# Adding negated row maxima to attention scores by accumulating DMAs, in 8 of 32 units of a cross-attention block

## The chip, the cores and the metric

The kernel runs on one core of a Trainium2 chip. The core has TensorE (PE), VectorE (DVE), ScalarE (ACT), GpSimd (POOL), the sync engine (SP), which here issues every DMA, and 16 DMA engines. The metric is the device time of one execution in microseconds (us), lower is better. All arithmetic is in float32.

## The reference

One transformer block with cross-attention over 8 sequences of 256 tokens, width 512, 16 heads of 32, and a context of 256 tokens for each sequence:

```python
x = layer_norm(hidden_states, ln1_w, ln1_b)
q = (x @ q_w + q_b)                      # split into 16 heads of 32
k = (encoder_hidden_states @ k_w + k_b)
v = (encoder_hidden_states @ v_w + v_b)
scores = einsum('bhqd,bhkd->bhqk', q, k) / sqrt(32)
scores = where(mask, scores, finfo.min)
attn = softmax(scores, axis=-1)
out = einsum('bhqk,bhkd->bhqd', attn, v) @ cproj_w + cproj_b
hidden = out + residual
y = gelu(layer_norm(hidden, ln2_w, ln2_b) @ fc_w + fc_b)
return hidden + (y @ proj_w + proj_b)
```

The part that matters here is the softmax: for each query and head the largest score over the 256 keys is subtracted before the exponential.

## The kernel before

The 8 sequences are worked in two groups (g = 0, 1) of four. Each group goes through the projections of context and tokens, the attention, the output projection, a second layer norm and the two large matrix products of the MLP. The projections and the MLP use recursive 2 x 2 block products with sums of blocks, so DVE and POOL compute many block sums (names such as `c1t`, `x1t`, `ows`, `pw0i`, `y0i`) that feed TensorE.

Attention is cut into 32 units. A unit is named by three digits: group, quarter of the heads (4 heads each), sequence within the group; unit 010 is group 0, head quarter 1, sequence 0. A unit goes through `scores` and `attend`:

- `s` (PE): 8 products give the scores of 4 heads, keys on the 128 partitions in two chunks, 256 queries in the free dimension.
- `ev` (ACT, L619): 8 evictions from PSUM, which also add the mask, into two tiles `pr0` and `pr1` of 128 x 1024 floats, two heads each. One tile of 512 KB is called a half below.
- `mx` (DVE, L1022), `mt` (DVE), `mc` (3 copies on ACT, L1029), `fold` (DVE, L1030): the maxima over the keys, which lie across partitions, end as 32 x 32 numbers (4 heads x 256 queries).
- `md` (SP, L1033): a store of these 4 KB to DRAM.
- `mm` (SP, L1035): a load that repeats the 1024 maxima on all 128 partitions, 128 x 1024 floats, 512 KB.
- `less` (L1038 to L1048): for each half, scores minus maxima in place; on POOL as two instructions of 128 x 512 (L1047), or on DVE as one of 128 x 1024 (L1042).
- `exp` (ACT, L1050): one exponential per half, in place.
- `av` (PE): products of the exponentials with ones (the denominators) and with the values; then DVE normalises.

What is executed in which order is written out by hand. `PROGRAM` is a list of some thousands of words, one for each step, such as `less010_0:G`: the step's name and, after the colon, the engine where there is a choice (V is DVE, A is ACT, G is POOL). The steps are issued in this order, so that on each engine, and on SP's queue, instructions stand in the order of the list and none overtakes another. `PLACES` gives each buffer its slot in SBUF or bank in PSUM. An exponential that waits on ACT therefore holds up every eviction behind it, and a wait on POOL or SP everything behind that. A unit's `av` stands about three units behind its `s` in TensorE's order.

Of the kernel before, what the change touches and what calls it, by code (L numbers as in the profile page):

```python
# [13 lines left out]
ALU = mybir.AluOpType  # L14
PSUM = bass.MemoryType.PSUM

P = 128
# [105 lines left out]

PROGRAM = """
# [42 lines left out]
less010_0:G stats_x1_30 mc012_2 k1_0_P4 k1_0_c12:A mm030 r002 mc012_1 kd0_1_11 mc012_3 ev032_21 mx032_0 ev032_30  # L167
k1_1_P2 ev032_31 less010_1:G ev032_20 k1_0_c21 exp010_0 fold012 k1_1_P3 mx032_1 md012 vd0_1_21 exp010_1 aggr_x1_30
# [8 lines left out]
r030 exp032_1 xb1_21 xb1_20 v1_1_t2:A att030 s003 less012_1:V v1_0_t2:A mm001 av032 xb1_01 mx021_0 ev003_20  # L177
ev003_11 xb1_22 ev003_21 xb1_23 ev003_10 mt021 ev003_00 v1_0_P5 ev003_31 r032 exp012_0 att032 ev003_30 mc021_1
v1_1_P5 mx003_1 mc021_2 ev003_01 less001_0:G mc021_3 exp012_1 fold021 s023 v1_0_c11 md021 v1_1_t3:A mx003_0 xb1_13
av012 xb1_10 ev023_00 less001_1:G ev023_01 mt003 v1_0_t3:V ev023_31 ev023_21 mc003_2 v1_0_P7 mc003_3 r012 ev023_20  # L180
ev023_30 mc003_1 ev023_10 att012 ev023_11 xT1_20 s011 exp001_0 fold003 mx023_0 md003 v1_1_P2 ev011_00 mm021
ev011_31 xb1_12 ev011_11 ev011_20 xb1_11 exp001_1 v1_1_P3 xb1_03 v1_1_c11 ev011_30 mx023_1 ev011_01 ev011_21
v1_0_P3 ev011_10 mt023 xT1_21 x1_20:A mx011_1 mc023_1 x1_21:A less021_1:G s031 mm003 mc023_2 v1_0_c22 mc023_3
v1_0_c12:A xb1_02 mx011_0 av001 xb1_00 ev031_11 ev031_00 less021_0:G mt011 xT1_10 mc011_2 ev031_30 fold023 mc011_3
v1_1_P7 ev031_01 xb1_32 r001 mc011_1 xb1_31 ev031_20 exp021_1 xb1_33 att001 fold011 less003_1:G v1_0_P4 ku033
ev031_31 xT1_11 md023 ev031_21 ev031_10 xb1_30 mx031_1 exp021_0 md011 s013 v1_1_c22 x1_10:A less003_0:G xT1_01
# [17 lines left out]
mx120_1 mm102 s110 o0_0_t1 o0_1_P6 ev110_30 mt120 pw0i1_2:G ev110_31 ev110_11 less100_0:V ev110_20 ev110_21 o0_0_P6  # L204
mc120_2 ev110_10 less100_1:G fold122 ev110_01 mx110_1 mc120_3 mc120_1 ev110_00 s130 o0_1_t2 fold120 pw0i1_4:G
o0_0_P2 ev130_21 o0_0_t2 md120 ev130_10 a0t4:V ev130_20 md122 ev130_11 fl002_0 ev130_01 o0_1_P5 ev130_00 pw0i1_3:V
mm120 exp100_1 mx110_0 ows4:G fl006_2 ev130_30 prd0_1_True o0_0_P5 less102_0:G exp100_0 o0_1_t3 fl001_2 mx130_0
ev130_31 av100 mx130_1 mm122 less102_1:G exp102_0 mt110 mt130 o0_0_t3 mc110_2 s112 mc130_2 r100 mc130_1 mc130_3
mc110_3 o0_1_P3 mc110_1 less120_1:G ev112_11 fold130 ev112_30 o0_0_c11 md130 ev112_31 ev112_21 att100 ev112_20
fold110 o0_0_P3 ev112_01 o0_1_c12 md110 ev112_10 less120_0:G ev112_00 mx112_1 pw0_01_00 exp102_1 o0_1_P7 mm130  # L210
o0_0_c12 exp120_1 mx112_0 less122_0:G mm110 exp120_0 o0_0_P7 o0_1_c22 stats_y0_31 hd3 mt112 s132 mc112_2 o0_0_c22
mc112_1 less122_1:G mc112_3 stats_y0_20 o0_1_P4 ev132_00 aggr_y0_31 fold112 ev132_11 stats_y0_30 ev132_31 md112
# [22 lines left out]
fc016_P2 y0i2_1:G fl002_3 fc012_c11 mm103 fc016_P6 pw0i5_2:G fc016_c11 fl002_1 y0i2_2:G fc002_t1 fc006_P6 pw0i5_4:G  # L235
mx123_0 s111 pw0i3_2:G prd0_5_True mx123_1 pw0i3_3:G fc002_P6 ev111_01 fl006_3 less121_1:G ev111_11 fc006_t2
ev111_10 fc012_P6 mt123 fc016_t2 mc123_3 fc002_P2 ev111_00 fc002_t2 mc123_2 fc006_P5 fl012_3 less121_0:V exp121_1
fc016_P5 mc123_1 fc002_c11 pw0i3_4:G exp121_0 fl006_1 fc002_P5 fold123 y0i6_3:G mx111_0 fc002_P7 md123 less103_0:G
prd0_3_True av121 fc012_t2 fl007_2 fc006_t3 fc016_t3 mm123 y0i2_4:G fc012_P5 fl015_0 fc002_t3 ev111_31 y0i6_4:G
ev111_30 fc002_c22 ev111_21 fc006_P3 less103_1:G ev111_20 exp103_0 mx111_1 fc006_P7 fc002_P4 mt111 fc006_c12  # L240
# [134 lines left out]
mm001=54 av030=2 r030=10 rc030=3 ku021=12 s021_0=1 s021_1=3 s021_2=4 s021_3=0 pr021_0=2 pr021_1=50 mx021=0 mm021=18  # L375
# [136 lines left out]
def tile_xattn_block(  # L512
# [59 lines left out]
    def at(b, i, n=1, w=256):  # L572

        return tile_of(b)[:, i * w : (i + n) * w]
# [42 lines left out]
    def copy(name, dst, src, to, of_, n, bias):  # L617
        T.op(name, [("ACT", 0.356 if n == 256 else 0.57)], [src, (cols, None)], [dst],
             lambda e: nc.scalar.activation(to(), of_(), AF.Identity, bias=bias(), scale=1.0))  # L619
# [389 lines left out]
    def scores(g, hg, b, halves):  # L1009
        u, q, k, v = operands_of(g, hg, b)  # L1010
        sb = [Buf(f"s{u}_{j}", "C", 2) for j in range(4)]
        mm(f"s{u}", 1.076, [(q[0], None), (k[0], None)], [(s, None) for s in sb], [
            (lambda kc=kc, j=j: at(sb[j], kc), lambda kc=kc, j=j: row(k, j)[:, ts(kc, P)], lambda j=j: row(q, j), True)
            for kc in range(2) for j in range(4)], mode="row")
        pr = [Buf(f"pr{u}_{h}", "Q", 4) for h in range(2)]
        for kc in range(2):
            for j in range(4):
                copy(f"ev{u}_{j}{kc}", (pr[j // 2], [2 * (j % 2) + kc]), (sb[j], [kc]), lambda j=j, kc=kc: at(pr[j // 2], 2 * (j % 2) + kc),
                     lambda j=j, kc=kc: at(sb[j], kc), 256, lambda kc=kc: col(2 * (4 * g + b) + kc))
        mx = Buf(f"mx{u}", "mx", 7)  # L1020
# [5 lines left out]
        T.op(f"mt{u}", [("DVE", 0.15)], [(mx, [0, 1])], [(mx, [2])], lambda e: nc.vector.transpose(tile_of(mx)[:, 64:128], tile_of(mx)[:, 0:64]))  # L1026
        for a in range(1, 4):
            T.op(f"mc{u}_{a}", [("ACT", 0.2)], [(mx, [2])], [(mx, [2 + a])],
                 lambda e, a=a: nc.scalar.copy(tile_of(mx)[0:32, 64 + 64 * a : 128 + 64 * a], tile_of(mx)[32 * a : 32 * a + 32, 64:128]))  # L1029
        T.op(f"fold{u}", [("DVE", 0.38)], [(mx, [2, 3, 4, 5])], [(mx, [6])], lambda e: nc.vector.tensor_reduce(  # L1030
            tile_of(mx)[0:32, 320:352], tile_of(mx)[0:32, 64:320].rearrange("p (m c) -> p c m", c=32), axis=mybir.AxisListType.X, op=ALU.max))
        md = dram(f"md{u}", [32, 32])
        store(f"md{u}", md, None, [(mx, [6])], lambda: md.t, lambda: tile_of(mx)[:32, 320:352], 0.01)  # L1033
        M = Buf(f"mm{u}", "Q")
        load(f"mm{u}", M, None, lambda: tile_of(M), lambda: md.t.rearrange("a r -> (a r)").partition_broadcast(P), 0.5, src=[(md, None)])  # L1035
        ss = Buf(f"ss{u}", "Q", 2) if halves else None
        for h in range(2):
            def less(e, h=h):  # L1038
                if e == "DVE":
                    p_ = tile_of(pr[h]).rearrange("p (i k q) -> p i k q", i=2, k=2)  # L1040
                    m_ = tile_of(M)[:, 512 * h : 512 * h + 512].rearrange("p (i q) -> p i q", i=2)
                    nc.vector.tensor_tensor(p_, p_, m_[:, :, None, :].to_broadcast([P, 2, 2, S]), ALU.subtract)  # L1042
                    return
                for i in range(2):
                    j = 2 * h + i
                    p_ = at(pr[h], i, 1, 512).rearrange("p (k q) -> p k q", k=2)
                    E[e].tensor_tensor(p_, p_, at(M, j)[:, None, :].to_broadcast([P, 2, S]), ALU.subtract)  # L1047
            T.op(f"less{u}_{h}", [("POOL", 2.448), ("DVE", 1.16)], [(pr[h], None), (M, None)], [(pr[h], None)], less, lock=True, pieces=2)  # L1048
            T.op(f"exp{u}_{h}", [("ACT", 0.947)], [(pr[h], None)], [(pr[h], None)],
                 lambda e, h=h: nc.scalar.activation(tile_of(pr[h]), tile_of(pr[h]), AF.Exp), table="exp")  # L1050
            if halves:
                two = lambda h=h: tile_of(pr[h]).rearrange("p (i k q) -> p i k q", i=2, k=2)
                plus(f"ss{u}_{h}", (ss, [h]), (pr[h], None), (pr[h], None), lambda h=h: at(ss, h, 1, 512).rearrange("p (i q) -> p i q", i=2),
                     lambda two=two: two()[:, :, 0, :], lambda two=two: two()[:, :, 1, :], 512, pool_too=True)
        return u, v, pr, ss

    def attend(g, hg, b, u, v, pt, ss):
        av = Buf(f"av{u}", "C")
        if ss:
            sums_ = [(lambda j=j: tile_of(av)[j * HD : (j + 1) * HD, 256:512], lambda: ones, lambda j=j: at(ss, j), True) for j in range(4)]  # L1060
        else:
            sums_ = [(lambda j=j: tile_of(av)[j * HD : (j + 1) * HD, 256:512], lambda: ones,
                      lambda j=j, kc=kc: at(pt[j // 2], 2 * (j % 2) + kc), kc == 0) for kc in range(2) for j in range(4)]
        mm(f"av{u}", 1.36 if ss else 1.72, [(v[0], None)] + ([(ss, None)] if ss else []) + [(p_, None) for p_ in pt], [(av, None)], sums_ + [
            (lambda j=j: tile_of(av)[j * HD : (j + 1) * HD, :256], lambda j=j, kc=kc: v[1]()[:, kc, j * HD : (j + 1) * HD],
             lambda j=j, kc=kc: at(pt[j // 2], 2 * (j % 2) + kc), kc == 0)
# [432 lines left out]
```

## Time and profile before

| | |
|---|---|
| runs of the kernel, us | 663.23 and 663.9, median 663.57 |
| span of the profiled execution, first to last instruction, us | 662.0 |
| median of the runs less that span, us | 1.6 |
| TensorE clock granted, share of full speed | 1.00 |
| `md`: issue on SP, median us | 0.32, 32 times |
| `exp`: 64 on ACT, mean us | 1.07 |

The profile shows one execution; its own time is its span and what lies around it, for which the last difference stands. Its page gives busy time by engine, the chain of work that ended last, and groups of instructions by line and engine with the names of the tiles that they write and read (`pr<-pr,mm` writes `pr` and reads `pr` and `mm`). Rows of a timeline read: start, duration, engine, line, operation, tiles, shapes, how many of them were merged, and in brackets the idle time of the engine before them and what ended it. Rows of a table by windows give a stretch, its length, the busy time and number of instructions of the five compute rows (PEld is TensorE's weight load), the clock, the share of the 16 DMA engines, and GB/s. SPq is SP's queue of DMA issues. The idle time of an engine that nothing waits for costs nothing.

### The profile page before, as it was taken

To read this page: it belongs to the slowest core of one execution; us is meant where nothing else is said; L and a number is where in the kernel's file an instruction comes from. 1 tells how busy PE (TensorE), PEld (TensorE's weight loads), DVE (VectorE), ACT (ScalarE), POOL (GpSimd) and SP (SyncE) were. 2 spreads that over 40 slices of the span, in tenths; PEclk is the share of its full clock that TensorE was granted. 3 is DMA by queue.
4 is the path that set the end of the run, shared out by engine and by line. 5 is a ranking of instruction groups with operands and counts; after the bars stand their busy time and mean duration, and the time that the engine had idled before them with its cause. 6 is when DMAs were issued, how large, how long until landed. Compare 5 with 4: busy or idle time off the path is not lost.

```text
span 662.0 us, 11469 instructions
## 1 busy us (share of the span) xinstructions
PE 654.6 (99%) x3925; PEld 490.0 (74%) x3925; DVE 585.7 (88%) x980; ACT 342.4 (52%) x702; POOL 374.8 (57%) x340
## 2 busy tenths in 40 slices
PE   8999999999999999999999999999999999999997
PEld 7746554477544776777688888888888888888887
DVE  2998799999999999999999998997789787998775
ACT  2046479799999899866995572030020013930000
POOL 1262773646888997699958774423535217720260
PEclk9999999999999999999999999999999999999999
DMA  8999888786574467886878698889978779359366
GB/s 250 311 356 307 211 197 291 267 255 125 144 241 161 144 202 234 263 268 197 266 249 273 198 235 225 289 269 230 195 193 241 190 201 242 93 142 240 106 141 111
DMA packets 206586, 144.84 MB, mean 219 GB/s; under 512 B 117008, under 2 KB 166976, under 8 KB 206528
## 3 DMA queue, kind: packets, MB, share of 16 engines
q1 hardware_dynamic: 206528, 144.11, 76.8%
q8 instruction: 31, 0.51, 0.3%
q14 instruction: 27, 0.22, 0.1%
HBM read 104.10 MB, written 39.98 MB: 218 GB/s over the span
## 4 chain that ended last, share of the span: by engine, by line
PE 92%; DVE 5%; ACT 1%; DMA 1%; issue 0%; SPq 0%; POOL 0%; DVEq 0%; ACTq 0%
PE pd_X L639 15%; PE fc_X L639 14%; PE fc_W L639 8%; PE av L639 7%; PE pd_W L639 7%; PE s L639 4%; PE o_X L639 4%; PE q_X L639 4%; PE k_X L639 4%; PE v_X L639 4%; PE pd_Y L639 4%; PE fc_Y L639 4%; PE q_W L639 2%; PE k_W L639 2%; PE v_W L639 2%; PE o_W L639 2%
## 5 line engine op out<-in xcount | busy, mean ns | idle before, releaser
L1047 POOL TENSOR_TENSOR pr<-pr,mm 128x512 f32<-128x512 f32 x84 | 110.4, 1346 | 22.8 <-DMA mm<-md 9.2
L619 ACT ACTIVATE pr<-s,cols 128x256 f32<-128x256 f32 x256 | 104.5, 482 | 21.8 <-PE s L639 15.8
L1022 DVE TRANSPOSE_TENSOR_REDUCE mx<-pr 128x32 f32<-128x1024 f32 x64 | 77.6, 1223 | 3.3 <-ACT pr L619 3.3
L1227 ACT ACTIVATE h<-h,cols 128x256 f32<-128x256 f32 x128 | 54.1, 498 | 36.7 <-DVE h L630 36.6
L1050 ACT ACTIVATE pr<-pr 128x1024 f32<-128x1024 f32 x64 | 66.9, 1069 | 3.4 <-POOL pr L1047 2.8
L630 DVE TENSOR_TENSOR h<-fc_X,h 128x512 f32<-128x512 f32 x80 | 52.8, 679 | 6.2 <-PE fc_X L639 5.5
L630 DVE TENSOR_TENSOR h<-fc_W,h 128x512 f32<-128x512 f32 x48 | 32.0, 679 | 5.8 <-PE fc_W L639 5.3
L639 PE MATMUL av<-pr,ones 128*32 128x256 f32 x512 | 34.2, 384 | 0.7 <-ACT pr L1050 0.6
L1029 ACT COPY mx<-mx 32x64 f32<-32x64 f32 x96 | 23.1, 243 | 19.8 <-DVE mx L1026 15.8
L1042 DVE TENSOR_TENSOR pr<-pr,mm 128x1024 f32<-128x1024 f32 x22 | 30.8, 1407 | 0.0
L628 POOL TENSOR_TENSOR z1i<-h,z1i 128x512 f32<-128x512 f32 x4 | 5.7, 1440 | 40.4 <-PE pd_X L639 40.4
L639 PEld LDWEIGHTS av<-pr,ones 128*32 128x32 f32 x512 | 14.1, 109 | 18.5 <-issue 6.7
L630 POOL TENSOR_TENSOR h<-h,fl 128x512 f32<-128x512 f32 x9 | 11.5, 1295 | 24.6 <-DVE fl L630 15.0
L639 PE MATMUL fc_W<-y1i,fl 128*128 128x256 f32 x100 | 24.6, 380 | 0.0
L639 PE MATMUL fc_X<-y1i,fl 128*128 128x256 f32 x88 | 21.6, 381 | 0.0
L639 PEld LDWEIGHTS fc_W<-y1i,fl 128*128 128x128 f32 x100 | 18.9, 190 | 2.9 <-DVE h L630 0.3
L639 PE MATMUL pd_W<-z0i,pl 128*128 128x256 f32 x88 | 20.6, 379 | 0.0
L1030 DVE TENSOR_REDUCE mx<-mx 32x32 f32<-32x256 f32 x32 | 18.4, 574 | 1.4 <-ACT mx L1029 1.3
L639 PE MATMUL pd_X<-z0i,pl 128*128 128x256 f32 x80 | 18.9, 379 | 0.0
L606 ACT COPY fl<-fc_X 128x512 f32<-128x512 f32 x6 | 3.5, 580 | 29.5 <-PE fc_X L639 29.2
L639 PEld LDWEIGHTS fc_X<-y1i,fl 128*128 128x128 f32 x88 | 16.6, 190 | 2.6 <-ACT h L606 0.2
L639 PEld LDWEIGHTS pd_W<-z0i,pl 128*128 128x128 f32 x88 | 16.7, 190 | 2.3
(595 smaller groups left out, 1815.6 us busy)
## 6 DMA issues: line engine op xcount, KB each, us to landing
mm<-md SPq DMA_DIRECT2D x32, 512.0 KB, 5.1
pl<-prd SPq DMA_DIRECT2D x47, 256.0 KB, 4.2
fl<-fcd SPq DMA_DIRECT2D x41, 256.0 KB, 4.0
fl<-prd SPq DMA_DIRECT2D x24, 256.0 KB, 3.8
fw<-in_L_xattn_fc_w_dram SPq DMA_DIRECT2D x16, 256.0 KB, 4.9
pw<-in_L_xattn_proj_w_dram SPq DMA_DIRECT2D x32, 128.0 KB, 3.6
hid<-in_x_dram SPq DMA_DIRECT2D x8, 512.0 KB, 4.8
hd<-hid SPq DMA_DIRECT2D x8, 512.0 KB, 3.4
```

What stands on the lines that cost most here:

```text
L606: (nc.scalar.copy if e == "ACT" else nc.vector.tensor_copy)(to(), of_())
L619: lambda e: nc.scalar.activation(to(), of_(), AF.Identity, bias=bias(), scale=1.0))
L628: nc.gpsimd.tensor_tensor(to()[:, ts(k, 512)], in0()[:, ts(k, 512)], in1()[:, ts(k, 512)], op)
L630: E[e].tensor_tensor(to(), in0(), in1(), op)
L639: nc.tensor.matmul(o(), l(), r(), start=first, stop=True, skip_group_check=True)
L1022: T.op(f"mx{u}_{h}", [("DVE", 1.126)], [(pr[h], None)], [(mx, [h])], lambda e, h=h: nc.vector.tensor_reduce(tile_of(mx)[:, 0:64].rearrange ...
L1029: lambda e, a=a: nc.scalar.copy(tile_of(mx)[0:32, 64 + 64 * a : 128 + 64 * a], tile_of(mx)[32 * a : 32 * a + 32, 64:128]))
L1030: T.op(f"fold{u}", [("DVE", 0.38)], [(mx, [2, 3, 4, 5])], [(mx, [6])], lambda e: nc.vector.tensor_reduce(tile_of(mx)[0:32, 320:352], tile_ ...
L1042: nc.vector.tensor_tensor(p_, p_, m_[:, :, None, :].to_broadcast([P, 2, 2, S]), ALU.subtract)
L1047: E[e].tensor_tensor(p_, p_, at(M, j)[:, None, :].to_broadcast([P, 2, S]), ALU.subtract)
L1050: lambda e, h=h: nc.scalar.activation(tile_of(pr[h]), tile_of(pr[h]), AF.Exp), table="exp")
L1227: lambda e, f=f, b=b, c=c: nc.scalar.activation(at(h[f][b], c), at(h[f][b], c), AF.Gelu_apprx_tanh, bias=col(c_fcb + f * 4 + c), scale=1.0 ...
```

## The change

In eight units, named in `ADDING`, the load `mm` is gone and so are the subtractions. In their place POOL issues for each half a DMA that reads 16 of the 32 rows of maxima from DRAM (512 numbers, for two heads), repeated on 128 partitions and for the two key chunks, and adds them to the half in SBUF (`accum_op=ALU.add`). So that adding is right, `fold` now writes negated maxima, and the other 24 units add instead of subtracting. So that 512 numbers in a row fit, a half is ordered by key chunk first and head second (it was head first), in the evictions, the maxima, the exponentials' users and the `less` of all units. All 16 changed `less` steps were on POOL before, and each keeps its place in the list; the eight `mm` words are taken out. Nothing else in `PROGRAM` moves, and `PLACES` stays.

```diff
+ADDING = "010 001 021 003 102 120 122 103".split()
...
-less002_1:V kd0_1_21 mm010 exp002_0 k1_1_P5 mx012_1 kd0_1_22 ev012_11 ku001 exp002_1 att020 av022 mt030 xt1_1
+less002_1:V kd0_1_21  exp002_0 k1_1_P5 mx012_1 kd0_1_22 ev012_11 ku001 exp002_1 att020 av022 mt030 xt1_1
...
-                copy(f"ev{u}_{j}{kc}", (pr[j // 2], [2 * (j % 2) + kc]), (sb[j], [kc]), lambda j=j, kc=kc: at(pr[j // 2], 2 * (j % 2) + kc),
+                copy(f"ev{u}_{j}{kc}", (pr[j // 2], [2 * kc + j % 2]), (sb[j], [kc]), lambda j=j, kc=kc: at(pr[j // 2], 2 * kc + j % 2),
...
-                tile_of(mx)[:, 0:64].rearrange("p (k j q) -> p j k q", k=2, j=4)[:, 2 * h : 2 * h + 2],
+                tile_of(mx)[:, 0:64].rearrange("p (k j q) -> p k j q", k=2, j=4)[:, :, 2 * h : 2 * h + 2],
...
-            tile_of(mx)[0:32, 320:352], tile_of(mx)[0:32, 64:320].rearrange("p (m c) -> p c m", c=32), axis=mybir.AxisListType.X, op=ALU.max))
+            tile_of(mx)[0:32, 320:352], tile_of(mx)[0:32, 64:320].rearrange("p (m c) -> p c m", c=32), axis=mybir.AxisListType.X, op=ALU.max, negate=True))
...
+        adding = u in ADDING
         M = Buf(f"mm{u}", "Q")
-        load(f"mm{u}", M, None, lambda: tile_of(M), lambda: md.t.rearrange("a r -> (a r)").partition_broadcast(P), 0.5, src=[(md, None)])
+        if not adding:
+            load(f"mm{u}", M, None, lambda: tile_of(M), lambda: md.t.rearrange("a r -> (a r)").partition_broadcast(P), 0.5, src=[(md, None)])
...
             def less(e, h=h):
+                m_ = at(M, 2 * h, 2)
                 if e == "DVE":
-                    p_ = tile_of(pr[h]).rearrange("p (i k q) -> p i k q", i=2, k=2)
-                    m_ = tile_of(M)[:, 512 * h : 512 * h + 512].rearrange("p (i q) -> p i q", i=2)
-                    nc.vector.tensor_tensor(p_, p_, m_[:, :, None, :].to_broadcast([P, 2, 2, S]), ALU.subtract)
+                    p_ = tile_of(pr[h]).rearrange("p (k n) -> p k n", k=2)
+                    nc.vector.tensor_tensor(p_, p_, m_[:, None, :].to_broadcast([P, 2, 512]), ALU.add)
                     return
-                for i in range(2):
-                    j = 2 * h + i
-                    p_ = at(pr[h], i, 1, 512).rearrange("p (k q) -> p k q", k=2)
-                    E[e].tensor_tensor(p_, p_, at(M, j)[:, None, :].to_broadcast([P, 2, S]), ALU.subtract)
-            T.op(f"less{u}_{h}", [("POOL", 2.448), ("DVE", 1.16)], [(pr[h], None), (M, None)], [(pr[h], None)], less, lock=True, pieces=2)
+                for k in range(2):
+                    p_ = at(pr[h], k, 1, 512)
+                    E[e].tensor_tensor(p_, p_, m_, ALU.add)
+            def added(e, h=h):
+                m_ = md.t[16 * h : 16 * h + 16].rearrange("a r -> (a r)").partition_broadcast(P)
+                nc.gpsimd.dma_start(tile_of(pr[h]).rearrange("p (k n) -> p k n", k=2), m_[:, None, :].to_broadcast([P, 2, 512]), accum_op=ALU.add)
+            if adding:
+                T.op(f"less{u}_{h}", [("POOL", 1.0)], [(pr[h], None), (md, None)], [(pr[h], None)], added)
+            else:
+                T.op(f"less{u}_{h}", [("POOL", 2.448), ("DVE", 1.16)], [(pr[h], None), (M, None)], [(pr[h], None)], less, lock=True, pieces=2)
```

Two places show what this does to POOL's queue. The numbers behind a tile's name are those of its buffer; `x2` is two instructions. The first place is unit 010 (`pr_0_972`, `pr_1_959`) in group 0: before,

```order
L628 TENSOR_TENSOR c1t_1223<-c_10_966,c1t_1027 128x512 x2
L1047 TENSOR_TENSOR pr_0_972<-pr_0_972,mm_1142 128x512 x2
L1047 TENSOR_TENSOR pr_1_959<-pr_1_959,mm_1142 128x512 x2
L807 TENSOR_TENSOR rs_x_3_1294<-rs_x_3_1294,neg_half 128x2
L1047 TENSOR_TENSOR pr_1_1079<-pr_1_1079,mm_1250 128x512 x2
```

and now:

```order
L628 TENSOR_TENSOR c1t_1221<-c_10_966,c1t_1027 128x512 x2
L1051 DMA pr_0_972<-md_150 128x2x512
L1051 DMA pr_1_959<-md_150 128x2x512
L807 TENSOR_TENSOR rs_x_3_1289<-rs_x_3_1289,neg_half 128x2
L1048 TENSOR_TENSOR pr_1_1079<-pr_1_1079,mm_1247 128x512 x2
```

Four subtractions became two issues at the same place; they still stand behind the sums `c1t`, and wait for `md` instead of `mm`. The second place is POOL at units 102 (`mm_2327`), 120 (`mm_2410`) and 122 (`mm_2449`) in group 1, with units 130 and 110 behind them: before,

```order
L630 TENSOR_TENSOR ows_2414<-v_1_11_299,ows_2202 128x512
L1047 TENSOR_TENSOR pr_0_2216<-pr_0_2216,mm_2327 128x512 x2
L1047 TENSOR_TENSOR pr_1_2170<-pr_1_2170,mm_2327 128x512 x2
L1047 TENSOR_TENSOR pr_1_2299<-pr_1_2299,mm_2410 128x512 x2
L1047 TENSOR_TENSOR pr_0_2286<-pr_0_2286,mm_2410 128x512 x2
L1047 TENSOR_TENSOR pr_0_2111<-pr_0_2111,mm_2449 128x512 x2
L1047 TENSOR_TENSOR pr_1_2115<-pr_1_2115,mm_2449 128x512 x2
L1047 TENSOR_TENSOR pr_0_2395<-pr_0_2395,mm_2519 128x512 x2
L1047 TENSOR_TENSOR pr_1_2391<-pr_1_2391,mm_2519 128x512 x2
```

and now:

```order
L1051 DMA pr_0_2199<-md_189 128x2x512
L1051 DMA pr_1_2153<-md_189 128x2x512
L1051 DMA pr_1_2282<-md_188 128x2x512
L1051 DMA pr_0_2269<-md_188 128x2x512
L1051 DMA pr_0_2094<-md_190 128x2x512
L1051 DMA pr_1_2098<-md_190 128x2x512
L1048 TENSOR_TENSOR pr_0_2376<-pr_0_2376,mm_2492 128x512 x2
L1048 TENSOR_TENSOR pr_1_2372<-pr_1_2372,mm_2492 128x512 x2
```

Six halves are now issued one right behind the other, with no other work of POOL between them.

More of the change, by code (lines that the diff above doesn't have):

```diff
@@ L1051, in scores @@
             if halves:
[L1052 removed]
+                two = lambda h=h: tile_of(pr[h]).rearrange("p (k i q) -> p k i q", i=2, k=2)
                 plus(f"ss{u}_{h}", (ss, [h]), (pr[h], None), (pr[h], None), lambda h=h: at(ss, h, 1, 512).rearrange("p (i q) -> p i q", i=2),
[L1054 removed]
+                     lambda two=two: two()[:, 0], lambda two=two: two()[:, 1], 512, pool_too=True)
         return u, v, pr, ss
@@ L1062, in attend @@
             sums_ = [(lambda j=j: tile_of(av)[j * HD : (j + 1) * HD, 256:512], lambda: ones,
-                      lambda j=j, kc=kc: at(pt[j // 2], 2 * (j % 2) + kc), kc == 0) for kc in range(2) for j in range(4)]
+                      lambda j=j, kc=kc: at(pt[j // 2], 2 * kc + j % 2), kc == 0) for kc in range(2) for j in range(4)]
         mm(f"av{u}", 1.36 if ss else 1.72, [(v[0], None)] + ([(ss, None)] if ss else []) + [(p_, None) for p_ in pt], [(av, None)], sums_ + [
             (lambda j=j: tile_of(av)[j * HD : (j + 1) * HD, :256], lambda j=j, kc=kc: v[1]()[:, kc, j * HD : (j + 1) * HD],
-             lambda j=j, kc=kc: at(pt[j // 2], 2 * (j % 2) + kc), kc == 0)
+             lambda j=j, kc=kc: at(pt[j // 2], 2 * kc + j % 2), kc == 0)
             for kc in range(2) for j in range(4)], mode="col")
```

41 lines of the change are left out of this document (20 added, 21 removed).

## The prediction

> **What bounds the kernel now.** I read the page first: busy times, then the chain that ended last.
>
> ```profile
> span 662.0 us, 11469 instructions
> ...
> PE 654.6 (99%) x3925; PEld 490.0 (74%) x3925; DVE 585.7 (88%) x980; ACT 342.4 (52%) x702; POOL 374.8 (57%) x340
> ...
> PE 92%; DVE 5%; ACT 1%; DMA 1%; issue 0%; SPq 0%; POOL 0%; DVEq 0%; ACTq 0%
> ```
>
> TensorE works 654.6 of 662.0 us and makes 92% of the chain; POOL, from which the change takes work, makes 0%. All that any relief can bring is TensorE's idle time, 662.0 - 654.6 = 7.4 us. So the question is whether something that TensorE waits for comes later. For that I read the stretches in which the eight units run: first all attention from 99 to 265 us, then the four places where the changed units stand, and one stretch with a single load of maxima in it.
>
> ```profile
> core 0: us, PE busy (x) PEld busy (x) DVE busy (x) ACT busy (x) POOL busy (x), PEclk, DMA share, GB/s
> 99.00:265.00 166.00, 164.83 (x1383) 100.50 (x1382) 159.21 (x278) 153.89 (x319) 121.44 (x93) 1.00 0.69 207
> ...
> 218.00:222.00 4.00, 4.00 (x30) 3.04 (x29) 4.00 (x6) 2.70 (x9) 4.00 (x4) 1.00 0.42 131
> 119.00:129.00 10.00, 10.00 (x59) 4.63 (x61) 9.93 (x23) 7.43 (x17) 8.45 (x8) 1.00 0.87 288
> 143.00:170.00 27.00, 26.94 (x259) 18.89 (x261) 24.91 (x43) 26.43 (x59) 14.02 (x12) 1.00 0.72 139
> 228.00:245.00 17.00, 17.00 (x132) 13.06 (x135) 16.81 (x30) 14.47 (x33) 17.00 (x14) 1.00 0.75 233
> 299.00:312.00 13.00, 13.00 (x95) 9.66 (x97) 12.76 (x23) 8.96 (x14) 12.76 (x14) 1.00 0.69 197
> ```
>
> TensorE is idle for 1.2 us of these 166. ACT is busy for 153.9 of them (93%), so ACT cannot make good several us in which it stands at a wait. The second number from the end is the share of the DMA engines: they are no empty road, 0.69 to 0.87 at the four places.
>
> **The change part by part.** The rows of the work that goes, and of the queue that issues it:
>
> ```profile
> L1047 POOL TENSOR_TENSOR pr<-pr,mm x84: 1258/1278/2767, 85.1 to 318.2; 128x512 f32<-128x512 f32 x84
> L593 SPq DMA_DIRECT2D mm<-md x32: 319/344/889, 79.2 to 367.8; - x32
> ...
> DMA to landing us min/median/max: 3.4/5.1/7.2
> ...
> DMA to landing us min/median/max: 3.7/3.7/3.7
> ...
> SPq L593 <- DMA md<-mx: 8.3, 9, 1.9
> ```
>
> *Removed on POOL:* 8 units x 4 subtractions x 1.28 = 41 us. No piece of it is on the chain, and TensorE has no gap behind it: worth 0. *Removed on SP:* 8 issues of 0.34 us and at most the 8.3 us that SP spent at its nine waits for maxima; what was queued behind starts earlier, but TensorE has no gap that it ended: 0. *Changed in the other 24 units:* the order of a score tile, the sign, an add for a subtraction, on the same shapes, one POOL call per key chunk in place of one per head. If each of the 52 POOL calls left took the 0.02 us between minimum and median more or less, that is 1 us on POOL, beside TensorE's work: 0.
>
> *Added:* 16 DMAs, two per unit, each writing half a unit's scores, 128 x 1024 numbers or 512 KB. No row shows an accumulating DMA or one that POOL issues. The nearest is the load it replaces: also 512 KB, from the same small tensor. The one at 218.0 us has the engines almost to itself: it lands after 3.7 us, and 4 us x 0.42 = 1.68 us of that is time of all engines; the other 2.0 are fixed. Bounds for the data time of one adding half: 1.68 us if the add is free, 5.0 us if read, read and write each cost a plain copy. I take 3.36, twice the load, since it must read two sources, maxima and scores, where the load read one. For POOL's issue the ends are SP's 0.34 us and the 2.55 us of the two calls it replaces; I take 1.0, nearer to SP's row, since it is an issue. While other packets are there, an adding packet twice as long that alternates with a plain one takes 1.5 times as long; with a share b of other traffic I multiply by 1 + b/2.
>
> [...] No row of the trace shows an add.
>
> *Unit 010.* POOL comes to it at 119.46, behind sums that waited for ACT; below it ACT's two exponentials, three copies of maxima behind them, and TensorE's use (start, duration, engine, line):
>
> ```profile
> 119.46 4.97 POOL L1047 TENSOR_TENSOR pr<-pr,mm 128x512 f32<-128x512 f32 x4
> ...
> 122.77 1.07 ACT L1050 ACTIVATE pr<-pr 128x1024 f32<-128x1024 f32 x1
> 124.46 1.06 ACT L1050 ACTIVATE pr<-pr 128x1024 f32<-128x1024 f32 x1 [0.62 <-POOL pr L1047]
> 126.08 0.75 ACT L1029 COPY mx<-mx 32x64 f32<-32x64 f32 x3 [0.56 <-DVE mx L1026]
> ...
> 127.87 1.07 PE L639 MATMUL av<-pr,ones 128*32 128x256 f32 x16
> ```
>
> With b = 0.87 a half takes 3.36 x 1.43 = 4.8 us. The first lands at 119.5 + 1.0 + 2.0 + 4.8 = 127.3, the second at 132.1; its exponential ends at 133.2, and TensorE starts 5.3 us late. ACT stands at the first exponential from 122.8 on, and behind it wait the copies for unit 032 and the evictions of the next scores, so later units move with it, not further. Ends: 0 (data as in the load, issue as on SP: ready at 127.7) and 12 (5.0 us of data, 2.55 of issue: 139.5).
>
> *Units 001, 021, 003.* Here POOL waited for the load itself:
>
> ```profile
> 149.31 4.99 POOL L1047 TENSOR_TENSOR pr<-pr,mm 128x512 f32<-128x512 f32 x4 [7.01 <-ACT pr L619]
> 160.52 4.99 POOL L1047 TENSOR_TENSOR pr<-pr,mm 128x512 f32<-128x512 f32 x4 [6.22 <-DMA mm<-md]
> ...
> 143.37 0.49 SPq L593 DMA_DIRECT2D mm<-md  x1
> ...
> 155.18 1.05 ACT L1050 ACTIVATE pr<-pr 128x1024 f32<-128x1024 f32 x1
> ...
> DMA to landing us min/median/max: 2.9/4.5/5.6
> ...
> 172.81 3.66 PE L639 MATMUL q_X<-x,qw 128*128 128x512 f32 x8
> ```
>
> Unit 001's maxima were in DRAM by 143.4, when SP issued the load; POOL was idle and now issues then. The first half lands at 143.4 + 3.0 + 3.36 x 1.27 = 150.7, before its exponential at 155.18; the later two gain their load in the same way: 0. But six halves are 20.2 us of the engines for three loads' 5.0, 15 more in a stretch of 27 that had 7.6 free. With them compete the loads of the normalised tokens (the last landing row, median 4.5 us), whose product starts at 172.81 with nothing idle before it. Between 0 and another 4.5 us I take 2, nearer to 0, since the adds here have room and can be the ones that wait.
>
> *Units 102, 120, 122.* POOL's 18 calls in one row are these units and 130 and 110 behind them:
>
> ```profile
> 227.82 22.28 POOL L1047 TENSOR_TENSOR pr<-pr,mm 128x512 f32<-128x512 f32 x18
> ...
> 230.36 1.06 ACT L1050 ACTIVATE pr<-pr 128x1024 f32<-128x1024 f32 x1 [1.07 <-POOL pr L1047]
> ...
> 235.62 3.22 ACT L1050 ACTIVATE pr<-pr 128x1024 f32<-128x1024 f32 x3
> ...
> 243.71 2.05 ACT L1050 ACTIVATE pr<-pr 128x1024 f32<-128x1024 f32 x2
> ...
> 247.40 1.07 PE L639 MATMUL av<-pr,ones 128*32 128x256 f32 x16
> ```
>
> POOL issues six halves from 227.8 on, faster than they move. They need 20.2 us; the other traffic is 0.75 x 17 less two loads of 1.68, or 0.55. The sixth lands at 227.8 + 3.0 + 20.2 x 1.28 = 256.6, its exponential ends at 257.7, and the product of unit 122, at 247.40 until now, is 10.3 us late. POOL is free 9 us earlier for unit 130, but its exponentials stand behind these on ACT. Ends: 0 and 24, by the same two prices.
>
> *Unit 103.*
>
> ```profile
> 299.34 2.52 POOL L1047 TENSOR_TENSOR pr<-pr,mm 128x512 f32<-128x512 f32 x2
> ...
> 303.20 2.50 POOL L1047 TENSOR_TENSOR pr<-pr,mm 128x512 f32<-128x512 f32 x2
> ...
> 306.47 1.06 ACT L1050 ACTIVATE pr<-pr 128x1024 f32<-128x1024 f32 x1
> ...
> 311.20 1.07 PE L639 MATMUL av<-pr,ones 128*32 128x256 f32 x16
> ```
>
> The halves land at 299.3 + 3.0 + 4.3 = 306.6 and, behind it on the engines, 310.9; the exponential ends at 312.0, 0.8 us late.
>
> Sum: 5.3 + 2 + 10.3 + 0.8 = 18.4, about 19 with the small waits between. The profiled execution spans 662.0; the two runs shown have a median of 663.57, 1.6 more, which I add: 662 + 19 + 1.6 = 682.6, rounded to 682.
>
> **Rivals.** *The transfer is hidden (not slower).* If the add is free, a half is 1.68 us of data. Unit 010 then lands at 124.9 and 127.3, 0.5 late; the six halves are there by 243.7, in time; with ACT standing 2.6 us at 230.4 the sum is about 2: 665.6. It decides at the six halves: they are in time as long as 227.8 + 3.0 + 6 x d x 1.28 stays under 247.4 - 1.1, that is up to d = 2.0 us. For it: the load lands in 5.1 us at the median with other traffic. Against it: scores are read as well. [...]
>
> *Dearer.* Three copies' time (5.0 us) and 2.55 us of POOL per issue: unit 010 ends at 139.5 (12 late), the six halves at 271.9 (24 late), unit 103 at 317.8 (7 late), the token loads 4.5: +47, about 711. For it: no row bounds how fast POOL describes such a transfer. [...]
>
> *A gain.* Freed POOL and SP fill TensorE's gaps: at most the 1.2 us of this stretch if no add comes late: 662.4. Units 001 to 003 are so placed, 010 and 122 are not.
>
> **How the numbers follow.** A measurement of this kernel tells 2% from no change, 650.3 to 676.8. Twice the load (682, its own range 672 to 692): 0.42; hidden: 0.30; dearer: 0.22, spread from 692 to 730; a gain: 0.06. Slower takes the dearer case and four fifths of the likeliest: 0.56. Faster would need more than TensorE's idle time: 0.01. Same: 0.43. The range runs from 662, which leaves out most of the gain (0.05), to 706, which leaves out somewhat over half of the dearer case (0.12).
>
> **What would show it.** In the profile after: a second DMA queue with 16 issues by POOL of about 1 us; their landing, 6 to 8 us for a first half and 4 to 5 more for each one behind it; ACT waiting for DMA before exponentials near 123 and 230; TensorE gaps before the products of units 010 and 122, of some 5 and 10 us; no gap for 001. If those gaps are missing, the data time was under 2.0 us and the kernel stays near 665; if POOL's issue takes over 2 us or a half over 5, it goes to 700 and over.

## The result and the profile after

The kernel after takes 694.7 us (median of two runs, 694.88 and 694.53). Against the kernel before its ratio is 1.047, 95% interval 1.044 to 1.050: slower, by 31 us, where 682 was predicted with a range of 662 to 706. The profiled execution took 694.88 us and spans 693.1, which is 31.1 more than the 662.0 before.

The page of the kernel after: span, busy times, the two DMA queues, and the chain of work that ended last.

```profile
span 693.1 us, 11467 instructions
...
PE 664.2 (96%) x3925; PEld 494.5 (71%) x3925; DVE 590.8 (85%) x980; ACT 343.1 (49%) x702; POOL 355.1 (51%) x324
...
q1 hardware_dynamic: 205376, 139.92, 71.5%
q0 software_dynamic: 4352, 8.39, 7.1%
...
PE 52%; DMA 3%; DVE 2%; POOL 1%; issue 1%; ACT 1%; SPq 0%; POOLq 0%; DVEq 0%; ACTq 0%
```

The chain is no measure of the loss here: it could be followed back only to 280.7 us, so its shares add up to 60% and can't be set against the 92% before. TensorE's busy time rises by 9.6 us, though the trace has the same 3925 of its matmul instructions, and its idle time from 7.4 to 28.9. So about 21.5 of the 31.1 us are idleness, and the rest is slower work. Queue q0 is new: the 16 DMAs of POOL. The next view is TensorE's waits, the longest first (engine, tile and line, what was waited for, total us, times, longest).

```profile
PE av L639 <- ACT pr L1057: 7.3, 4, 3.1
PE q_X L639 <- ACT x L762: 4.6, 1, 4.6
PE o_W L639 <- DVE hid L630: 4.0, 1, 4.0
PE av L639 <- ACT pr L619: 3.3, 2, 2.1
```

The first row is waits of a product `av` for an exponential (L1057 is now the exponential's line). Two of its four, 3.1 and 2.5 us, are the forecast gap of unit 010, and one of 1.2 us is unit 103's; the gap forecast before unit 122's product is not among them. The longest single waits are elsewhere: before the first product of the queries, and before a product `o_W` of the output projection, which reads no scores at all. In the last row 2.1 us are unit 130's. The slower work shows in a table by windows, whose third number from the end is the granted clock.

```profile
130.54:137.37 6.83, 3.81 (x30) 1.55 (x32) 1.72 (x2) 4.29 (x9) 0.00 (x0) 0.50 0.51 160
185.15:191.98 6.83, 5.83 (x7) 2.53 (x8) 6.55 (x11) 6.76 (x15) 5.36 (x4) 0.50 0.59 156
256.83:263.66 6.83, 5.23 (x12) 4.21 (x13) 6.52 (x10) 6.46 (x14) 0.00 (x0) 0.50 1.14 206
```

In three gaps the clock falls to half for 6.83 us; in the kernel before it was 1.00 from 6 us to 661 us. TensorE worked 14.9 us at half clock, so an estimate of the loss is 7.4 of the 9.6 us. Last, the DMAs themselves (issue durations on POOL, who waited, issue to landing) and, in a second view, the loads of the normalised tokens, which took 2.9/4.5/5.6 us to land before.

```profile
L1051 POOL DMA_DIRECT2D pr<-md x16: 1201/1688/3720, 119.5 to 328.1; - x16
...
  ACT pr L1057: 25.0, 7
...
DMA to landing us min/median/max: 6.9/11.3/20.0
```

```profile
L593 SPq DMA_DIRECT2D xb<-xd x16: 331/684/6382, 150.4 to 184.0; - x16
...
DMA to landing us min/median/max: 4.0/8.2/12.6
```

ACT stood 25.0 us at seven exponentials, each time for one of these DMAs. How late TensorE is along the program, by the start of the same product in both timelines:

| product of unit | before | after | later by | added since the row above |
|---|---|---|---|---|
| 030, behind 010 | 136.17 | 144.25 | 8.1 | 8.1 |
| 003 | 176.40 | 192.66 | 16.3 | 8.2 |
| 100 | 229.63 | 247.77 | 18.1 | 1.9 |
| 110, behind 102, 120, 122 | 254.56 | 281.62 | 27.1 | 8.9 |
| 121, ahead of 103 | 300.51 | 327.13 | 26.6 | -0.4 |
| 123, behind 103 | 317.12 | 346.84 | 29.7 | 3.1 |
| end of the span | 662.0 | 693.1 | 31.1 | 1.4 |

Units 010 (first row) and 001, 021 and 003 (second row) were to cost 5.3 and 2, units 102, 120 and 122 10.3, unit 103 0.8.

### The profile page after: what moved, and what is told of

Read it like the earlier page. It is cut to its first block, busy times and chain, and to the rows that moved or that the text cites. A ratio compares the mean times of both kernels' runs of the same rounds, so it can differ in the third digit from the quotient of the medians.

```text
span 693.1 us, 11467 instructions
## 1 busy us (share of the span) xinstructions
PE 664.2 (96%) x3925; PEld 494.5 (71%) x3925; DVE 590.8 (85%) x980; ACT 343.1 (49%) x702; POOL 355.1 (51%) x324
## 3 DMA queue, kind: packets, MB, share of 16 engines
q0 software_dynamic: 4352, 8.39, 7.1%
## 4 chain that ended last, share of the span: by engine, by line
PE 52%; DMA 3%; DVE 2%; POOL 1%; issue 1%; ACT 1%; SPq 0%; POOLq 0%; DVEq 0%; ACTq 0%
PE pd_X L639 14%; PE fc_X L639 11%; PE pd_W L639 7%; PE fc_W L639 6%; PE pd_Y L639 3%; PE fc_Y L639 3%; PE o_X L639 2%; PE av L639 2%; DMA pr<-md 2%; PE o_W L639 1%; PE s L639 1%; DMA mm<-md 1%; PE o_Y L639 1%; ACT pr L1057 0%; POOL y0i L630 0%
## 5 line engine op out<-in xcount | busy, mean ns | idle before, releaser
L1048 POOL TENSOR_TENSOR pr<-pr,mm 128x512 f32<-128x512 f32 x52 | 71.4, 1400 | 33.3 <-DMA mm<-md 28.5
L1057 ACT ACTIVATE pr<-pr 128x1024 f32<-128x1024 f32 x64 | 66.9, 1064 | 26.5 <-DMA pr<-md 25.0
L639 PE MATMUL av<-pr,ones 128*32 128x256 f32 x512 | 36.8, 392 | 10.7 <-ACT pr L1057 7.3
L639 PEld LDWEIGHTS av<-pr,ones 128*32 128x32 f32 x512 | 14.6, 110 | 30.2 <-ACT pr L1057 10.3
L1051 POOL DMA_DIRECT2D pr<-md x16 | 20.2, 1861 | 12.3 <-PE s L639 10.9
```

The source lines that it names most:

```text
L639: nc.tensor.matmul(o(), l(), r(), start=first, stop=True, skip_group_check=True)
L1048: E[e].tensor_tensor(p_, p_, m_, ALU.add)
L1051: nc.gpsimd.dma_start(tile_of(pr[h]).rearrange("p (k n) -> p k n", k=2), m_[:, None, :].to_broadcast([P, 2, 512]), accum_op=ALU.add)
```

## The experiments

The theory is that all of the loss comes from halves that land late, place by place, because a transfer by POOL starts late, halves follow one another in series, other loads wait behind them, and what waits in order on ACT and DVE carries the delay to TensorE, whose clock then falls. Rivals: the new order and sign cost something everywhere; the places make one another worse; the add itself is the whole price. The kernel before, measured beside the experiments, had medians of 664.8 to 666.3 us, with single runs from 662.7 to 673.9, so results are given as ratios to it, and in us as ratio times 663.6.

### The layout alone, and one place at a time

Each of these five kernels differs from the kernel after in which units add by DMA; the others have their load `mm` and their `less` on POOL back, at the places of the kernel before.

```diff
-ADDING = "010 001 021 003 102 120 122 103".split()
+ADDING = "".split()                 # 1: layout and sign alone
+ADDING = "010".split()              # 2
+ADDING = "001 021 003".split()      # 3
+ADDING = "102 120 122".split()      # 4
+ADDING = "103".split()              # 5
```

> No unit adds by DMA: all 32 units load their maxima and add them with POOL or DVE, in the new order of a half and with the new sign. Theory (all of the 31 us comes from the halves that land late): the kernel stands at the time before, 663.6, between 662 and 666, TensorE's clock is 1.00 throughout. Rival (the new order or the sign costs time in the units that don't change, for instance a slower add on POOL, 1.40 us in the kernel after against 1.28 before): at least 668.

> Only unit 010 adds by DMA. Theory (each place pays for its own late landing, read from the kernel after): TensorE is 8 us late behind the product of unit 010, of which 3.2 are a clock of 0.5 for 6.8 us: 671.7, between 670 and 674. Rival (the places make each other worse, a single one is taken up by slack): under 668. By the prediction's term alone: 669.

> Only units 001, 021 and 003 add by DMA. Theory (the token loads share the DMA engines with four adding halves and land 4 us and more later, TensorE waits for them before the product of the queries, and its clock then falls): 672, between 669 and 675, one gap of 3 to 5 us before the first query product. Rival (the waits there come from ACT, already late from unit 010): under 667 without that gap. By the prediction's term alone: 665.6.

> Only units 102, 120 and 122 add by DMA. Theory (ACT stands some 8 us at the first exponential of unit 102, the copies of maxima behind it and DVE's queue stand too, TensorE waits for DVE, then for unit 122): 674, between 671 and 676, with one stretch of clock 0.5. Rival (the delay there is inherited from the two places before it): under 668. By the prediction's term alone: 673.9.

> Only unit 103 adds by DMA. Theory (each place pays for its own late landing; in the kernel after, its second half landed 11.7 us after its issue and TensorE was 3.7 us late from there on): span 666, between 664.5 and 667, ratio 1.005. Rival (what was seen there is inherited from the places ahead): span under 664. By the prediction's term alone: 663.1.

| units that add | ratio, interval | us more than before | TensorE later at the place, by the timelines |
|---|---|---|---|
| none | 1.001 (0.998 to 1.004) | 0.5 | 0 |
| 010 | 1.013 (1.009 to 1.018) | 8.9 | 8.6 |
| 001, 021, 003 | 1.014 (1.009 to 1.018) | 9.0 | 6.1 |
| 102, 120, 122 | 1.013 (1.007 to 1.019) | 8.7 | 8.3 |
| 103 | 1.006 (1.002 to 1.009) | 3.7 | 5.0 |

The last column is by how much TensorE's lateness grows between two products, one ahead of the place and one behind it: 002 and 030, 012 and 003, 100 and 101, and, for unit 103, 121 and the end.

The layout and the sign cost nothing that can be measured. The four places add up to 30.3 us, with intervals of 2 to 4 us each, and the kernel after loses 31.1. So each place pays for itself, and nothing shows that the places make one another worse; a few us of that would not stand out. In the third kernel the time was as expected, but the gap, 2.9 us long, was not before the queries' product but before a `scores` product; that one waited for DVE, and DVE stood 7.4 us at the transposition of the token loads. The token loads landed after 3.2/7.0/15.0 us. (Its two columns differ because the profiled execution, 670.9 us, was the shortest of four, 670.9 to 675.4.) In the fourth the time was as expected too, but behind DVE's 3.3 us TensorE waited 2.6 us before unit 130's product, not for unit 122. The profiled execution of the kernel with 103 alone spans 672.3 us, by a stall at 216 us far ahead of unit 103 (last section); its 5.0 us are counted from behind that stall.

### Two halves fewer beside the token loads

```diff
-ADDING = "001 021 003".split()
+ADDING = "001 021".split()
```

> Only units 001 and 021 add by DMA: the two halves of unit 003 are taken out of the kernel that adds in 001, 021 and 003 (ratio 1.014, span 668.7). Theory (the loads of the normalised tokens wait behind adding halves; with two halves fewer, 5 to 6 us of the engines' time come free before 172): the token loads issued near 160 land within 9 us where two of them took 15 and 11.5, TensorE's gap before the scores at 169.7 is under 1 us, clock 1.00, span 663 to 665. Rival (unit 001 or 021 alone holds ACT or DVE up): 667 or more.

Measured: 1.008 (1.005 to 1.011), 5.2 us; token loads 3.3/7.2/11.2 us; clock 1.00; one gap of 1.2 us before the queries' product, and TensorE 2.9 us later at the place where three units made 6.1. With two halves fewer the delay is smaller, as the theory has it, and the gap before the scores is under 1 us (0.4), but the delay does not go away. The span, 667.3, missed the expected 663 to 665 and lies in the rival's range; 1.5 and 1.0 us of it were lost near 210, where nothing adds.

### A copy in place of the add

```diff
-nc.gpsimd.dma_start(tile_of(pr[h])..., m_..., accum_op=ALU.add)
+nc.gpsimd.dma_start(tile_of(pr[h])..., m_...)
...
-lambda e, h=h: nc.scalar.activation(tile_of(pr[h]), tile_of(pr[h]), AF.Exp), table="exp")
+lambda e, h=h: nc.scalar.activation(tile_of(pr[h]), tile_of(pr[h]), AF.Exp, scale=0.001 if adding else 1.0), table="exp")
```

> The kernel after, all eight units, with the 16 DMAs of POOL copying the maxima over the scores where they added them (the sum of scores and maxima is left out in these units, and their exponentials take a thousandth of the value so that they stay finite; shapes, queues, waits and order are the same). Theory (a half's 2.8 us of data is the add: packets of 2 KB that take 176 ns against 84 for a plain one): packets fall to about 85 ns, halves follow each other by 1.4 us, the last of the six lands some 10 us earlier, and the time falls from 694.7 to about 680, between 674 and 686; what is left of the 31 us is the fixed part of a transfer issued by POOL and the order on ACT. Rival 1 (the software queue sets the pace, the add is free): packets or their spacing stay, 692 to 697. Rival 2 (the fixed part counts for nothing): under 670.

Measured: 1.030 (1.024 to 1.037), or 683.5 us, as expected. The page's row of the software queue and the rows of its issues:

```profile
q0 software_dynamic: 2304, 8.39, 5.0%
...
L1051 POOL DMA_DIRECT2D pr<-md x16: 722/722/867, 120.9 to 321.3; - x16
...
  ACT pr L1057: 20.1, 5
...
DMA to landing us min/median/max: 5.8/10.1/13.3
```

The copy moves a half in 128 packets of 4 KB, the add in 256 of 2 KB. In the packet records a copying packet takes 159 ns undisturbed (169 at the median) and an adding one 176, so by an estimate a half alone is 1.3 us of all 16 engines against 2.8. The six halves of 102, 120 and 122 end 1.3 us apart at the close (landings 256.4, 257.7, 259.0, 260.5) where adding halves ended 2.6 apart, and the last lands 13.3 us after its issue in place of 20.0, or 16.9 us after the first issue in place of 23.6: 6.7 us sooner, not 10. So the add costs an estimated 1.5 us a half, 24 us of the engines in all (by the two pages' shares of the queue, 7.1% of 693.1 us and 5.0% of 685.9, its packets took 49 and 34 us of them, 15 apart), and of the 31 us lost it accounts for 11, or 7 to 15 by the copy's interval. The other 20 stay when the add is gone. Three things are in them that no run separates: the fixed part of the transfer, the waits in order, and the bytes, since two halves of 512 KB are moved for each unit where the load `mm` moved 512 KB once (8.39 MB on the new queue, 4.19 fewer on the old one). Even beside copies the token loads land after 3.1/9.3/11.0 us. By the timelines the places cost 7.8, 4.0, 4.8 and 2.2 us with copies, against 8.1, 8.2, 8.9 and 3.1 with adds. At unit 010 the copy saves next to nothing: its first half still lands 9.6 us after its issue.

### ACT's order at units 102, 120 and 122

The timeline of the kernel after at unit 102's first exponential, ACT first, then DVE and TensorE:

```profile
246.92 0.51 ACT L619 ACTIVATE pr<-s,cols 128x256 f32<-128x256 f32 x1
255.11 1.06 ACT L1057 ACTIVATE pr<-pr 128x1024 f32<-128x1024 f32 x1 [7.68 <-DMA pr<-md]
256.18 1.29 ACT L1029 COPY mx<-mx 32x64 f32<-32x64 f32 x6
...
257.11 0.57 DVE L1030 TENSOR_REDUCE mx<-mx 32x32 f32<-32x256 f32 x1 [5.94 <-ACT mx L1029]
257.61 0.67 DVE L630 TENSOR_TENSOR hid<-o_Y,hid 128x512 f32<-128x512 f32 x1
...
258.43 1.19 PE L639 MATMUL o_W<-qw,a0t 128*128 128x256 f32 x2 [3.99 <-DVE hid L630]
```

ACT waits 7.7 us for the first half of unit 102. Behind it stand six copies of maxima of units 110 and 130, for them DVE's `fold`, behind that a sum that empties a PSUM bank, and for the bank TensorE. Unit 102's own product starts 18 us after its last exponential: nobody was in a hurry for it. Three kernels with 102, 120 and 122 alone change orders. The first moves one exponential:

```diff
-exp102_0 mt110 mt130 ... mc110_1 ... pw0_01_00 exp102_1 ...
+mt110 mt130 ... mc110_1 ... pw0_01_00 exp102_0 exp102_1 ...
```

> Only units 102, 120 and 122 add by DMA, as in the third single-place kernel (672.5, ratio 1.013), and one word is moved: the first exponential of unit 102 goes on ACT behind the copies of maxima of units 110 and 130 and the evictions of unit 112, to the place just before the second one. No DMA is moved. Theory (ACT's order carries the first half's lateness to work that has nothing to do with it): the gap before the product o_W and the low clock there are gone, the maxima of 130 and 110 are loaded 5 us earlier; what stays is unit 122, whose second half lands at 251 for a product due at 247.4: 668, between 666 and 670. Rival (the adds hold up the transfers beside them, not ACT's order): 671 to 674.

Measured: 1.014 (1.010 to 1.018), 672.9 us: no better, and in the rival's range. The gap before `o_W` is gone, and a gap of 6.1 us stands before the scores of unit 101, whose banks wait for evictions behind the exponentials: ACT now waits 0.7, 1.7, 1.6, 2.6 and 2.7 us at five halves. Moved back by itself, the first exponential only shifts ACT's waits to the halves that come 2.6 us apart. The second kernel reorders the issues too:

```diff
-less102_0 less102_1 less120_1 less120_0 less122_0 less122_1
+less122_0 less122_1 less120_1 less120_0 less102_0 less102_1
-exp102_0 (ahead of the copies) exp102_1 exp120_1 exp120_0 exp122_0 exp122_1
+exp122_0 exp122_1 exp120_1 exp120_0 ... exp130_1 exp130_0 exp102_0 exp110_1 exp102_1 exp110_0
```

> Only units 102, 120 and 122 add by DMA, with the six issues on POOL in the order in which TensorE needs the units (122, 120, 102 in place of 102, 120, 122), and the six exponentials in the same order on ACT, none ahead of the copies of maxima of 110 and 130; unit 102's two go behind those of unit 130. Same transfers, same queue. Theory (six halves of 2.6 us in series can be hidden, since unit 102 is needed 16 us after its exponentials): within 2 us of the time before, 664 to 667, no gap above 2 us and no low clock. Rival (the transfers' own length decides, six halves do not fit): 670 or more.

Measured: 1.007 (1.004 to 1.010), 668.4 us. In the profiled execution the clock is 1.00 throughout, and TensorE is 4.7 us later at the place in place of 8.3. So some 3.6 us, nearly half of the place's loss, go by order alone, less than expected. The times agree with that, but their intervals (1.004 to 1.010 and 1.007 to 1.019) overlap, so it rests on the two timelines. The third spreads the exponentials:

```diff
-exp122_0 exp122_1 exp120_1 ... mc112_3 ... exp120_0 ... exp130_1
+exp122_0 ... mc112_3 exp122_1 ... exp120_1 ... exp120_0 exp130_1
```

> Only units 102, 120 and 122 add by DMA, issued in the order of need as in the kernel before of that name (ratio 1.007, span 667.3, ACT idle 3.9 us at exponentials in three waits, then TensorE 2.3 us before the scores of unit 101, whose banks wait for evictions behind these). Now the exponentials stand further apart on ACT: 122's second behind the copies of maxima of 112, 120's first where 122's first stood before, 120's second just ahead of unit 130's. Theory (what remained was ACT standing at halves that follow each other every 2.6 us): ACT's waits for the added halves under 1.5 us, span 664 to 666, left over is unit 102's second half, which lands at 254.5 for a product due at 252.8. Rival (the transfers beside the adds, for units 130 and 110, are what is late): 667 or more.

Measured: 1.007 (1.004 to 1.011), 668.5 us. The waits of that stretch:

```profile
POOL pr L1048 <- DMA mm<-md: 14.1, 2, 11.8
...
PE av L639 <- ACT pr L1057: 3.7, 1, 3.7
ACT pr L619 <- POOL pr L1048: 3.4, 1, 3.4
```

ACT no longer waits for an adding half. Now POOL waits 11.8 us for the maxima of unit 130, ACT for POOL, and TensorE for an exponential that I had put behind that. The load for unit 110 landed 8.8 us after its issue (5.4 in the kernel before). Behind TensorE's gap of 3.7 us the clock was at half for 6.8 us. So the rival's range came true: the loads beside the adds are late too, though part of this wait is the new order's own.

### The clock

> The kernel after, with products that nobody reads put into three of TensorE's idle times: 10 before and 8 in the middle of unit 010's product, 14 before the first product of the queries, some 0.23 us each, with constants as operands. The halves still land when they did. Theory (the clock of 0.5 for 6.8 us behind a gap costs TensorE some 3.2 us each time): the low stretches at 130.5 and 185.2 are gone, the one at 257 stays, and the time falls by about 6 us to 688, between 686 and 691. Rival (the lost clock lies beside other waits, and the added products are more work): 694 to 699.

```diff
+if u == "010":
+    idle = (lambda: tile_of(av)[:, :256], lambda: ident.t, lambda: cb.t[:, :256], True)
+    sums_ = [idle] * 10 + sums_[:2] + [idle] * 8 + sums_[2:]
...
+if name == "q1_0" and p == 1:
+    items = [(lambda: tile_of(bank)[:, :256], lambda: ident.t, lambda: cb.t[:, :256], True)] * 14 + items
```

Measured: 1.052 (1.046 to 1.057). This is the rival's range, but the run tells little: each added product took 0.46 us, twice what I had reckoned, so they outlasted the gaps, and the later gaps moved; the eight in the middle also change unit 010's sums. The low clock at 130 was gone, others came at 180, 242 and 269. So it was tried again on the kernel with unit 010 alone:

```diff
+if u == "010":
+    sums_ = [(lambda: tile_of(av)[:, :256], lambda: ident.t, lambda: cb.t[:, :256], True)] * 12 + sums_
```

> Only unit 010 adds by DMA, as in the first single-place kernel (ratio 1.013, span 670.1, clock 0.5 from 130.4 to 137.2). Added are 12 products of constants that nobody reads, 0.46 us each, ahead of unit 010's product: TensorE starts them where it fell idle (126.8) and is done at about 132.4, still before the second half's exponential (133.6), so nothing real is held up. Theory (the clock that falls behind a gap costs TensorE about 3.3 us): the clock stays 1.00 and the span falls to about 667, between 666 and 668, ratio 1.008. Rival (the low clock costs nothing, since TensorE would wait anyway): span 670 or more.

TensorE behind the second half's exponential, first without the added products, then with them:

```profile
133.65 1.50 PE L639 MATMUL av<-pr,ones 128*32 128x256 f32 x10 [2.74 <-ACT pr L1057]
...
137.21 1.12 PE L639 MATMUL k_W<-c1t,vw 128*128 128x512 f32 x2
```

```profile
127.85 5.45 PE L639 MATMUL av<-cb,ident 128*128 128x256 f32 x24
...
134.42 0.84 PE L639 MATMUL av<-pr,ones 128*32 128x256 f32 x10 [0.56 <-ACT pr L1057]
...
136.27 1.13 PE L639 MATMUL k_W<-c1t,vw 128*128 128x512 f32 x2
```

The rest of unit 010's product takes 1.85 us at full clock against 3.56, so the clock cost 1.7 us here, about half of the 3.8 us that TensorE works in such a stretch, not the 3.3 expected. The clock stays at 1.00, and by the timelines TensorE is 6.6 us late behind the place, where it was 8.6 without them. The time, 1.011 (1.005 to 1.016), does not tell it from the 1.013 without, and the span, 671.0, lies in the rival's range, as the profiled execution lost another 2.5 us near 210. The loss at the other two places, 2.9 and 2.6 us by the same halving, is an estimate that no run tried.

## Why the prediction came out as it did

Right: slower, in the range, by late halves at the places named; removals on POOL and SP worth nothing; layout and sign worth nothing (1.001). A POOL issue of 1.0 us was near: 1.2 to 1.3 for the first of a row, and 0.7 to 0.9 from the start of one to the next (the longer durations in the view overlap). The data of a half, twice a plain copy, holds: 2.8 us where 3.36 was taken, and 2.2 times the copy by the same queue.

Alone the four places cost 8.9, 9.0, 8.7 and 3.7 us by the ratios, where the terms were 5.3, 2, 10.3 and 0.8. Wrong, and together the 12 us by which the time exceeds the forecast (the sum was 682.6, which rounds to 683; the first two points are steps that the terms of the places contain):

- *The fixed 3.0 us from POOL's issue, 1.0 + 2.0.* By the packet records five issues found POOL's queue empty. What lies ahead of the first packet and behind the last was 2.3 to 2.9 us at units 001, 021 and 103, so the 3.0 was near, but 4.4 at unit 102 and 7.0 at unit 010 (5.1 before the first packet, 1.9 behind the last). First halves landed after 6.9 to 10.5 us, where 7.3 to 7.8 was forecast. What delays unit 010 is open: the copy's first packet started after 2.7 us there, and its half still landed after 9.6.
- *No term for the clock.* Gaps were priced at their length. By the estimate half clock adds 7.4 us to them.
- *Units 001, 021 and 003, term 2.* It rested on adds that "can be the ones that wait". They did not: the halves of 021 and 003 landed 2.9 to 4.1 us apart, and the other loads waited. The token loads' median went from 4.5 to 8.2 us, the longest from 5.6 to 12.6, beyond the bound of another 4.5, and DVE stood 6.6 us in three waits for them and ACT 5.9 us in two, with the work in order behind them. The prediction's own 15 us of data for 7.6 us of free engines had spoken against so small a term. The place cost 8.2, of which 2.9 is the estimate for the clock.
- *Unit 103, term 0.8.* The second half landed 13.9 us after the first one's issue, not 11.6. POOL issued it 2.2 us later, with other work between the two, as the prediction's own rows (299.34 and 303.20) had it. It cost 3.1 there, and 1.4 more was lost behind it.
- *Unit 010, term 5.3.* The second half landed 1.4 us later than forecast, and by the estimate the half clock added 1.9: 8.1 in all.

Units 102, 120 and 122 cost 8.9 against 10.3, and that the number is near is luck, since the step behind it was wrong. The term let the sixth half hold up unit 122. The sixth half landed 23.6 us after the first issue, not 28.8: the halves came 2.6 us apart where 4.3 was reckoned, and it was the other loads that waited (from 246 to 264 us POOL's queue had 87% of the engines' time). That adding and plain packets alternate, on which the factor 1 + b/2 rested, was an estimate of mine that no run shows. In the trace TensorE has no gap over 0.4 us before unit 122's product. Its loss there is the 4.0 us before `o_W`, 2.6 by the estimate for the clock, and 2.1 before unit 130's product, where ACT waited for POOL and POOL for late maxima. It began at the first half, by ACT's order, and the experiment that changed only orders won 3.6 of the 8.3 us that the place costs alone by the timeline.

The rival "hidden" had its point of decision wrong. It was to hold up to 2.0 us of data per half; the copy has 1.3, and still loses 20 us. So the data time of a half alone did not decide. The fastest DMA of POOL landed here after 5.8 us, as a plain copy beside other traffic.

1.9 us of the loss lie between 192 and 247 us, where no unit adds. They came in some of the single-place executions too and not in others; what sets them off is open.

## What to carry to other kernels

Price a transfer that replaces a computation by its place in the order, not by its length: find the first instruction that waits for it, and what stands behind that one on ACT, DVE and POOL, though it needs none of the data. Count what waits beside the transfer, too: here the loads on the other queue paid. Where several transfers are issued in a row, issue them in the order in which they are needed, and put the waits behind the work of others. Where TensorE will stand for some us, allow for a fall of the clock: here gaps of 3.1, 4.6 and 4.0 us each came with 6.83 us at half clock, and one of 2.3 us, in the kernel in the order of need, with none.

## What was not expected of the hardware

The clock. In the kernel after it fell for 6.83 us in gaps of 3.1, 4.6 and 4.0 us, in the kernel with the exponentials spread for 6.8 us behind a gap of 3.7 us, and in the kernel with the copy behind one of 1.55 us. There, three stretches of 3.4 us:

```profile
174.12:177.54 3.42, 3.42 (x17) 2.64 (x15) 1.05 (x2) 3.37 (x9) 0.00 (x0) 1.00 1.08 215
177.54:180.95 3.41, 1.86 (x28) 1.12 (x30) 3.31 (x8) 2.05 (x3) 0.00 (x0) 1.00 1.03 181
180.95:184.37 3.42, 3.42 (x30) 1.69 (x23) 2.67 (x5) 1.62 (x4) 0.00 (x0) 0.50 1.12 153
```

TensorE is idle for 1.55 us of the middle stretch, works again from 179.35, and the clock falls at the stretch's end. The falls in the kernel after, at 130.54, 185.15 and 256.83, lie 54.61 and 71.68 us apart, 16 and 21 times 3.41 us. In the 3.41 us just ahead of each of them TensorE is idle for 2.56, 3.41 and 2.40 us. Of the other stretches at full clock on that grid, from 99 to 345 us, the one from 273.90 to 277.31 has the most idle time, 1.29 us, and no fall follows it. These are few falls, and in the kernel in the order of need TensorE was idle for 2.07 us of the 3.40 from 244.80 without one. What sets a fall off, and what makes it last 3.4 or 6.8 us, is open.

DVE and POOL. In the profiled execution of the kernel with 103 alone, one sum on DVE took 5.79 us, beside three pairs of sums on POOL; in the kernel with 102, 120 and 122 it took 0.88.

```profile
213.99 5.79 DVE L630 TENSOR_TENSOR pw0i<-pw 128x256 f32<-128x256 f32 x1
...
212.12 2.49 POOL L628 TENSOR_TENSOR a0t<-att,att 128x512 f32<-128x512 f32 x2
214.58 2.48 POOL L628 TENSOR_TENSOR a0t<-att,a0t 128x512 f32<-128x512 f32 x2
217.03 2.47 POOL L628 TENSOR_TENSOR a0t<-att,att 128x512 f32<-128x512 f32 x2
```

It ends 0.3 us after POOL's last one, at 219.50, and TensorE lost 4.3 us to it. In the kernel before, the same sum, at 214.66 and beside the same three pairs (212.53 to 220.16), took 0.65 us. So lying beside POOL's sums did not by itself make it slow, and what held it in the one execution no run here shows.
